# A graph-and-mixture kernel: last scan chunk unpaired, its tail work re-timed, and the spare-tile condition moved ahead of the first mixture

## The chip, the cores and the metric

The kernel runs on one core of one Trainium2 chip. The metric is device time in microseconds (us), the median over timed runs of one launch. A core has five engines, each with a queue of its own that it works through in order: TensorE (PE, matmuls; PEld is its weight load), VectorE (DVE), ScalarE (ACT), GpSimd (POOL) and SyncE (SP, which here only issues transfers). A wait at the head of a queue holds everything behind it.

## The reference

Two layers on 4096 tokens of width 256. Each has a graph part and a mixture of experts, both added to the input. What matters here, cut down:

```python
def step(hst, inp):                       # the scan over the tokens
    dAt, dBut, Ct = inp
    hst = dAt * hst + dBut                # 512 channels x 16 states
    return (hst, hst @ Ct)
y = (ys + u * D_skip) * silu(z)
# layer 0
h = layernorm(relu(adj @ x_n @ gcn_w + gcn_b))
x = x + mamba(h) @ w_out                  # the scan sits in here
xf = layernorm(x)                         # first mixture: 8 experts, the best 2 of each token
probs = softmax(xf @ gate_w + gate_b)
x = x + sum over the best 2:  probs_e * (gelu(xf @ W1_e + b1_e) @ W2_e + b2_e)
# layer 1
x = x + relu(new_adj @ (tanh(x_n @ W_proj + b) @ W_gcn) + b)
x = x + second mixture                    # 6 experts, the best 2, three layers each
```

The reference computes every expert on every token; the kernel only those that were chosen.

## The kernel before

**Stages.** The scan of layer 0 runs first, to about 1296 us of the span; then routing for the first mixture, the first mixture, the propagation of layer 1, the second mixture and the output.

**The scan.** The tokens are cut into 8 chunks of 512. Each chunk takes 32 steps (n = 0 to 255 over all chunks; c is the chunk and i the step in it); a step treats one block of 128 channels and two of the 16 states. In each step POOL forms `db` (L1058), ScalarE the two decays `da` (`decay`, L1066), VectorE runs the two scans (`scan`, L1073) and multiplies by C into `hc` (`product`, L1083). Then the two states are to be summed up. In a *paired* step (`pair`, L1087) POOL issues a transfer that adds the second half of `hc` onto the first, and PE adds one half into the sum `psy` (`total`, L1100). In an unpaired step there is no transfer and PE adds both halves. When a block's last group is in, VectorE multiplies the sum by the gate `zs` (`gate`, L1109). All steps but the last four (252 to 255) are paired. The loop calls `total` for step n-3 and `gate` for step n-4; what is then left over is done after the loop.

**The work that runs beside the scan.** The order of the instructions on PE, VectorE, ScalarE and POOL inside the scan is written out by hand. `Front` prepares the next chunk. From step i = 8 of chunk 6 on, the tails run (`Tail`): for each chunk and each half of it (two token tiles), three steps: product(0), product(1) (L861 and L865, into `ps_out`, for which there is one buffer), then `put`: ScalarE copies the result to `xr` (L870), SP writes it to `x1d`, and ScalarE forms the mean and the squares (L876, L880, reading `ps_out`). `Norm` turns the result into normalised tokens and gate logits, one chunk after the other: fetch, normal (L913), turn (L924, L932) and logits (L936, L940); a piece goes to the steps in `NPIECES` of chunk 7, at `7 + 3 * c + d`. The roots and shifts of the deviations (L893, L902) stand in `NORMS`, at steps 1, 2, 18 and 19. `Last` does the same for chunk 7: `first` at steps 29 and 30, then `add` (L983) and `norm` after the loop (L997 to L1030), where the last logits are copied by L1028 and the residual rows by L1030.

**Routing.** `Dispatch` handles the choice. `choose` (with `router`, L98 to L126) takes the two best experts of each token tile, `place` (L209 to L244) gives every chosen row its place in its expert's list and ends with one-hot rows (L249, eight tiles' worth of columns each). There are two batches of token tiles: the first 28, then the last 4. `tables` (L262 to L348) then makes the number of tiles `d_tiles` (L270), the expert of each tile `d_exps` (L313), the bias of each tile (`d_b`, L332 and L336), the source rows `d_src` (L326) and the destination rows `d_dst` (L348). The second mixture uses the same class with eight batches of 4 tiles.

**The mixtures.** `expert_tiles` runs tiles of 256 rows that belong to one expert. For the first mixture up to 39 tiles can be needed (4096 x 2 rows and 8 experts). Per tile: POOL fetches the rows (`fetch`, L354), SP loads the weights and bias (L452, L455), PE transposes (L459), VectorE copies (`xkT`, L463), PE multiplies (L438), ScalarE applies the function (`hk`, L442), PE multiplies again (L423), VectorE adds the bias (L428) and POOL scatters the rows (`put`, L362). The first 36 tiles always run; the last three stand in a condition behind them:

```python
most = 2 * N // TR + dp.E // 2
tiles = nc.values_load(dp.tiles[0:1, 0:1], min_val=1, max_val=dp.K)   # L480
run(0, most)
with tc.If(tiles > most):                                              # L482
    run(most, dp.K)
```

`combine` (L490, L496) then gathers the two results of each token and adds them with their weights. The second mixture runs 37 tiles and has no condition.

Of the kernel before, what the change touches and what calls it, by code (L numbers as in the profile page):

```python
# [10 lines left out]
BF16 = mybir.dt.bfloat16  # L11
# [7 lines left out]
P = 128  # L19
CW = 512  # L20
TPC = CW // P
# [6 lines left out]
def kernel(ctx: ExitStack, tc: tile.TileContext, out: bass.AP, **a):  # L28
# [115 lines left out]
    def after(later, earlier):  # L144
        tc.add_manual_dep(
            later.ins, earlier.ins.name,
            mybir.DependencyInfo(mybir.DependencyClass.Sync, mybir.DependencyReason.DATA),
            reason="rows written by several transfers",
        )

    class Dispatch:
# [4 lines left out]
        def __init__(self, pool, E, name, batches):  # L156
# [6 lines left out]
            self.hi = pool.tile([P, 2 * NT], F32, name=f"{name}_hi")  # L163
            self.lo = None
            self.src = pool.tile([P, self.C], I32, name=f"{name}_src")
            self.dst = pool.tile([P, self.C], I32, name=f"{name}_dst")
# [33 lines left out]

        def place(self, b, psum, tag, pool, lo_pool):

# [41 lines left out]
            nc.vector.tensor_copy(self.hi[:, g0:g0 + G], rowi)  # L244
            if self.lo is None:
                self.lo = lo_pool.tile([P, 2 * NT, P], BF16, name=f"{self.name}_lo", bufs=1)
            S = 2 * TPC
            for g in range(0, G, S):
# [5 lines left out]
        def tables(self, psum, tp, biases):  # L254
# [70 lines left out]
            nc.vector.tensor_scalar(tok, tok, -1.0, 0.0, ALU.add, ALU.max)  # L325
            nc.vector.tensor_copy(self.src, tok)  # L326

            out = []
            for n, b in enumerate(biases):
                bk = self.pool.tile([P, b.shape[2], K], F32, name=f"{name}_b{n}")  # L330
                for m in range(b.shape[2]):
                    nc.vector.tensor_tensor(  # L332
                        tmp, ge[:, :, :E],
                        b[:, :, m].unsqueeze(1).to_broadcast([P, K, E]), ALU.mult,
                    )
                    nc.vector.tensor_reduce(bk[:, m, :], tmp, AX.X, ALU.add)  # L336
                out.append(bk)
# [44 lines left out]
    class Route:  # L382

        def __init__(self, dp, psum, tags, pool, lo_pool, fm, source, hidden, w, bias_b):
            self.dp, self.psum, self.tags, self.pool, self.lo_pool = dp, psum, tags, pool, lo_pool
            self.source, self.hidden, self.w, self.bias_b = source, hidden, w, bias_b
            self.ps = {}
            self.fm = fm  # L390
# [18 lines left out]
        def choose(self, b):  # L409
            dp, E = self.dp, self.dp.E  # L410
            logits = self.ps.pop(b)[:, :TPC * E].rearrange("p (t e) -> p t e", e=E)
            dp.choose(b, logits, self.bias_b, True, small)
            dp.place(b, self.psum, self.tags[2], small, self.lo_pool)

    def expert_tiles(dp, psum, pool, weights, bias_out, layers, kb_out, spare):
# [62 lines left out]

        most = 2 * N // TR + dp.E // 2
        tiles = nc.values_load(dp.tiles[0:1, 0:1], min_val=1, max_val=dp.K)  # L480
        run(0, most)
        with tc.If(tiles > most):  # L482
            run(most, dp.K)

    def combine(dp, pool, c, src, dst):
# [25 lines left out]
    with ExitStack() as s1:  # L511
# [43 lines left out]
        gate_b = load_bcast(const, a["L0_ffn_gate_b"], "gate_b")  # L555
        dp = Dispatch(r0, E0, "d0", [NT - TPC, TPC])

# [269 lines left out]
        class Tail:  # L827
# [3 lines left out]
            def __init__(self, c, hh, kept=None):  # L831
                self.c, self.hh, self.kept = c, hh, kept
                self.xr = None
                self.todo = [lambda: self.product(0), lambda: self.product(1), self.put]

            @staticmethod
            def step(tails):
                if tails:
                    tails[0].todo.pop(0)()
                    if len(tails) > 1 and tails[1].xr is None:  # L840
                        tails[1].fetch()
                    if not tails[0].todo:
                        tails.pop(0)
# [23 lines left out]
            def put(self):  # L867
                s0 = self.c * TPC + 2 * self.hh
                for j in range(2):
                    nc.scalar.activation(  # L870
                        self.xr[:, j, :], self.ps[:, j, :], AF.Identity,
                        accum_out=sums[:, s0 + j:s0 + j + 1],
                    )
                rows = tokens(x1d[self.c], 0)[:, 2 * self.hh:2 * self.hh + 2, :]
                nc.sync.dma_start(rows, self.xr)
                nc.scalar.activation(  # L876
                    nmean[:, s0:s0 + 2], sums[:, s0:s0 + 2], AF.Identity, scale=-1.0 / D
                )
                for j in range(2):
                    nc.scalar.activation(  # L880
                        self.ps[:, j, :], self.ps[:, j, :], AF.Square,
                        bias=nmean[:, s0 + j:s0 + j + 1], accum_out=ssq[:, s0 + j:s0 + j + 1],
                    )
# [60 lines left out]
        B0 = NT // 2  # L944
        NORMS[18] = lambda: Norm.root(B0, NT - TPC - B0)
        NORMS[19] = lambda: Norm.shift(B0, NT - TPC - B0)
        NPIECES = {}
        for c in range(NC - 1):
            nm = Norm(c)
            for d, piece in ((-2, nm.fetch), (0, nm.normal), (1, nm.turn), (2, nm.logits)):  # L950
                NPIECES.setdefault(7 + 3 * c + d, []).append(piece)

        class Last:
# [34 lines left out]
            def norm(self):  # L988
# [5 lines left out]
                for hh in range(2):  # L994
# [27 lines left out]
                    for j in range(2):  # L1022
                        for k in range(DB):
# [3 lines left out]
                            )  # L1027
                    nc.scalar.copy(lgs[:, s0:s0 + 2, :], ps_l[:, t0:t0 + 2, :])  # L1028
                for hh in range(2):
                    nc.scalar.copy(self.xr[hh], self.ps[hh])  # L1030
                    rows = tokens(x1d[c], 0)[:, 2 * hh:2 * hh + 2, :]
                    nc.sync.dma_start(rows, self.xr[hh])

        class Step:
# [3 lines left out]
            def __init__(self, c, i):  # L1038
# [6 lines left out]

                self.paired = c * STEPS + i < NC * STEPS - 4

# [63 lines left out]
        with tc.manual_schedule(engines={  # L1111
# [34 lines left out]
            advance(left)  # L1146
            steps, tails, kept = [], [], {}
            for n in range(NC * STEPS):
# [32 lines left out]
                cur.product()  # L1181
                if n > 3:
                    steps[n - 4].gate()
                if n > 2:
                    steps[n - 3].total()
                if i < 8:
# [13 lines left out]
            n = NC * STEPS  # L1200
            for k in range(n - 3, n):
                steps[k].total()
            for k in range(n - 4, n):
                steps[k].gate()
# [3 lines left out]
        dp.lo = onehots  # L1208
        dp.choose(0, lgs[:, :NT - TPC, :], gate_b, False, ra)
        dp.place(0, ps_y, "psy", ra, None)  # L1210
        last.norm()
# [5 lines left out]
    with ExitStack() as s2:  # L1217
        with ExitStack() as st:
            tp = st.enter_context(tc.tile_pool(name="tiles0", bufs=2, reuse_waits="tile"))
            with ExitStack() as sr:  # L1220
                rp = sr.enter_context(tc.tile_pool(name="routing0", bufs=2, reuse_waits="tile"))
                ps_r = sr.enter_context(tc.tile_pool(name="ps_r0", bufs=2, space=PSUM, reuse_waits="tile"))
                dp.choose(1, lgs[:, NT - TPC:, :], gate_b, False, ra)
                dp.place(1, ps_r, "pl", ra, None)
                b1 = load(wp, a["L0_ffn_b1"], "b1")
# [31 lines left out]
        eb2 = load(keep1, a["L1_ffn_expert_b2"], "eb2")  # L1257
        dp1 = Dispatch(keep1, E1, "d1", [TPC] * NC)

        def route1(pool, psum, tags, fm):  # L1260
# [4 lines left out]

            return Route(dp1, psum, tags, pool, keep1, fm, x3, hidden, rw2, rb2)

# [254 lines left out]
```

## Time and profile before

| | us |
|---|---|
| median of 3 runs | 2531.24 (2530.56 to 2532.2) |
| the profiled run | 2528.41 |
| its span | 2526.6 |
| PE busy | 2253.9 (89%) |
| VectorE busy | 1652.0 (65%) |
| ScalarE busy | 1196.9 (47%) |
| POOL busy | 1158.9 (46%) |
| accumulating transfers L1087 | x252, 870 ns of POOL each |
| row fetches L354 / scatters L362 | x146 / x146 (two for each tile, both mixtures) |
| granted clock of PE, mean | 0.941 |

The span is the time from the first to the last instruction that the profile shows; the run is 1.8 us longer. A page of the profile gives for each group its line, engine, operation, tiles (out<-in) and shape, then how often it ran, its busy time, the mean of one and the engine's idle time before it with what ended it. A row of the timeline begins with the start and the duration; in brackets at its end stand the idle time of the engine before it and what released it. Where one row stands for several instructions (x2), the duration is that of all of them.

### The profile page before, as it was taken

What the parts mean: (1) busy time and instruction counts of PE and PEld (TensorE: products, weight loads), DVE (VectorE), ACT (ScalarE), POOL (GpSimd) and SP (SyncE); (2) the same over time, 40 slices, a digit from 0 to 9 for tenths busy, and PEclk for the clock granted to TensorE, in tenths of its full rate; (3) what the DMA queues carried; (4) which work ended last, traced back from release to release, by engine and by line L of the source; (5) the groups of instructions that cost most, each with busy time, mean ns of one, the idle gap of its engine ahead of it and who ended that gap; (6) DMA issues with size and microseconds to landing.
All of it is one profiled execution on the core that took longest, in us unless ns stands there. A gap on an engine that the chain in (4) does not pass through costs nothing. (4 is left out here: it accounts for less than half of the span.)

```text
span 2526.6 us, 25781 instructions
## 1 busy us (share of the span) xinstructions
PE 2253.9 (89%) x7976; PEld 1453.3 (58%) x7976; DVE 1652.0 (65%) x2322; ACT 1196.9 (47%) x2029; POOL 1158.9 (46%) x861
## 2 busy tenths in 40 slices
PE   5989999999999999897876999789999999859991
PEld 4765655656465656554545888645444444448881
DVE  4049999999999999978994111292666666552224
ACT  1146656574656566675632222154666665423330
POOL 1037776777777777756733555310000000026650
PEclk9999999999999999998877999899999999969996
DMA  6369999999899999988955777561444444238776
GB/s 201 92 185 234 242 265 234 264 231 271 221 270 230 259 247 238 270 242 224 283 156 183 235 228 233 168 211 50 142 142 142 142 148 147 98 113 246 245 241 212
DMA packets 307185, 516.91 MB, mean 205 GB/s; under 512 B 25808, under 2 KB 174928, under 8 KB 306144
## 3 DMA queue, kind: packets, MB, share of 16 engines
q1 hardware_dynamic: 256736, 410.81, 51.3%
q0 software_dynamic: 50304, 104.37, 19.8%
q8 instruction: 67, 1.10, 0.2%
q14 instruction: 78, 0.64, 0.1%
HBM read 406.29 MB, written 42.73 MB: 178 GB/s over the span
## 5 line engine op out<-in xcount | busy, mean ns | idle before, releaser
L1058 POOL TENSOR_TENSOR db<-du,bb 128x1024 f32<-128x1024 f32 x256 | 606.7, 2370 | 345.5 <-ACT state L1079 125.7
L1073 DVE TENSOR_TENSOR_SCAN db<-da,state,db 128x512 f32<-128x512 f32 x512 | 627.4, 1266 | 55.6 <-ACT da L1066 53.2
L613 PE MATMUL pt<-at,gn 128*128 128x256 f32 x2048 | 492.7, 393 | 33.2 <-DVE gn L80 26.2
L1066 ACT ACTIVATE da<-dt,negA 128x512 f32<-128x512 f32 x512 | 347.6, 691 | 360.2 <-DVE db L1073 358.1
L613 PEld LDWEIGHTS pt<-at,gn 128*128 128x128 f32 x2048 | 401.4, 197 | 164.4 <-issue 73.3
L1316 PE MATMUL pf<-f,gn 128*128 128x512 f32 x1024 | 449.4, 594 | 0.0
L1083 DVE TENSOR_TENSOR hc<-db,cb 128x1024 f32<-128x1024 f32 x256 | 331.6, 1295 | 18.4 <-PE psy L1100 0.4
L1316 PEld LDWEIGHTS pf<-f,gn 128*128 128x128 f32 x1024 | 191.8, 190 | 227.3 <-issue 226.4
L1100 PE MATMUL psy<-hc,ident 128*128 128x512 f32 x520 | 279.7, 624 | 41.7 <-DMA hc<-hc 40.9
L442 ACT ACTIVATE hk<-ps_h,d_b 128x256 f32<-128x256 f32 x292 | 138.4, 474 | 370.2 <-PE ps_h L438 352.7
L78 POOL TENSOR_TENSOR ln_rs<-ln_rs,mhalf 128x4 f32<-128x4 f32 x24 | 34.5, 1436 | 573.5 <-DVE ln_rs L77 573.5
L428 DVE TENSOR_TENSOR yk<-ps_y,bk 128x512 f32<-128x512 f32 x73 | 50.5, 692 | 376.1 <-PE ps_y L423 327.0
L1306 ACT ACTIVATE f<-f 128x1024 f32<-128x1024 f32 x128 | 135.4, 1058 | 200.2 <-DVE f L1305 177.4
L354 POOL DMA_INDIRECT xk<-d_xd,d_src x146 | 141.8, 971 | 190.7 <-PE ps_xt L459 82.3
L1087 POOL DMA_DIRECT2D hc<-hc x252 | 219.3, 870 | 0.2
L438 PE MATMUL ps_h<-xkT,wk 128*128 128x256 f32 x872 | 212.5, 387 | 0.0
L423 PE MATMUL ps_y<-wk,hk 128*128 128x256 f32 x872 | 210.4, 379 | 0.1
L1305 DVE TENSOR_SCALAR f<-at 128x1024 f32<-128x1024 f32 x128 | 88.1, 689 | 170.1 <-PE pf L1316 163.2
L362 POOL DMA_INDIRECT d_ys<-yk,d_dst x146 | 144.0, 987 | 109.6 <-DVE yk L428 75.8
L438 PEld LDWEIGHTS ps_h<-xkT,wk 128*128 128x128 f32 x872 | 161.3, 192 | 32.4 <-ACT hk L442 11.2
L423 PEld LDWEIGHTS ps_y<-wk,hk 128*128 128x128 f32 x872 | 162.9, 190 | 21.2 <-ACT hk L442 0.5
L1100 PEld LDWEIGHTS psy<-hc,ident 128*128 128x128 f32 x520 | 99.5, 198 | 105.4 <-DVE db L1073 38.1
(236 smaller groups left out, 2503.7 us busy)
## 6 DMA issues: line engine op xcount, KB each, us to landing
at<-in_adjT_dram SPq DMA_DIRECT2D x256, 512.0 KB, 4.1
bb<-bcd SPq DMA_DIRECT2D x128, 512.0 KB, 5.3
cb<-bcd SPq DMA_DIRECT2D x128, 512.0 KB, 5.0
hc<-hc POOLq DMA_DIRECT2D x252, 256.0 KB, 6.4
wk<-in_L_ffn_W_dram SPq DMA_DIRECT2D x72, 512.0 KB, 4.9
wk<-in_L_ffn_expert_w_dram SPq DMA_DIRECT2D x111, 256.0 KB, 4.1
yg<-d_ys SPq DMA_DIRECT2D x32, 512.0 KB, 5.1
yd<-us SPq DMA_DIRECT2D x6, 1024.0 KB, 8.1
```

The costliest lines, as they stand in the source:

```text
L354: nc.gpsimd.indirect_dma_start(out=xk[:, j, :], out_offset=None, in_=self.xd[:, :], in_offset=bass.IndirectOffsetOnAxis(ap=self.src[:, c:c ...
L362: s_ = nc.gpsimd.indirect_dma_start(out=self.ys[:, :], out_offset=bass.IndirectOffsetOnAxis(ap=self.dst[:, c:c + 1], axis=0), in_=yk[:, j, ...
L423: nc.tensor.matmul(ps[:, j, :], hT[:, m, j * P:(j + 1) * P], w[:, m, :], start=(m == 0), stop=(m == kb_out - 1),)
L438: nc.tensor.matmul(ps[:, j, :], w[:, d, m * P:(m + 1) * P], xT[:, d, :], start=(d == 0), stop=(d == DB - 1),)
L613: nc.tensor.matmul(pt[:, k, :], xl[:, j, k * P:(k + 1) * P], at[:, jj, :], start=(j == 0 and k == 0), stop=(j == NT - 1 and k == DB - 1),)
L1058: nc.gpsimd.tensor_tensor(self.db, self.f.du[self.half][:, self.mi:self.mi + 1, :].to_broadcast([P, 2, CW]), self.bb, ALU.mult,)
L1066: nc.scalar.activation(da, self.f.dt[self.half][:, self.mi, :], AF.Exp, scale=negA[:, self.m, n:n + 1])
L1073: nc.vector.tensor_tensor_scan(self.db[:, j, :], da, self.db[:, j, :], state[:, self.m, n:n + 1], ALU.mult, ALU.add,)
L1083: nc.vector.tensor_tensor(self.hc, self.db, self.cb, ALU.mult)
L1087: nc.gpsimd.dma_start(self.hc[:, 0, :], self.hc[:, 1, :], accum_op=ALU.add)
L1100: nc.tensor.matmul(f.psy[m], ident, self.hc[:, j, :], start=False, stop=(self.g == GS - 1 and j == last),)
L1316: nc.tensor.matmul(pf[:, k, :], gn[:, j, k * P:(k + 1) * P], f[:, jj, :], start=(j == 0), stop=(j == NT - 1),)
```

## The change

It has these parts:

1. No step of chunk 7 is paired. The totals of unpaired steps run up to step n-2 instead of n-3, and a gate is called one step after its total.
2. The mean and squares of a tail (`Tail.squares`) run at the start of the next call of `Tail.step`, that is one step later, behind that step's decays.
3. The second root and shift go from steps 18 and 19 to 19 and 20, and the pieces of `Norm` three steps later.
4. The batches of the first mixture are 24 and 8 token tiles instead of 28 and 4. The one-hot rows are a function of their own, called for both batches after the second `place`.
5. In `tables` the bias products are ordered behind `d_src`, in both mixtures.
6. In `Last.norm` the residual copies are ordered behind the copies of the logits.
7. In the first mixture 35 tiles always run, and the condition with the four spare tiles stands ahead of the first of them. The list of scatters that later work is ordered behind starts anew after it.

```diff
-        def place(self, b, psum, tag, pool, lo_pool):
+        def place(self, b, psum, tag, pool):
...
-            if self.lo is None:
-                self.lo = lo_pool.tile([P, 2 * NT, P], BF16, name=f"{self.name}_lo", bufs=1)
-            S = 2 * TPC
+            self.row[b] = row
+
+        def one_hot(self, b):
+            g0, G, S, row = 2 * self.t0[b], 2 * self.T[b], 2 * TPC, self.row.pop(b)
             for g in range(0, G, S):
...
-            nc.vector.tensor_copy(self.src, tok)
+            found = nc.vector.tensor_copy(self.src, tok)
...
-                    nc.vector.tensor_tensor(
+                    mul = nc.vector.tensor_tensor(
...
+                    if n == 0 and m == 0:
+                        after(mul, found)
...
-        most = 2 * N // TR + dp.E // 2
+        most = 2 * N // TR + dp.E // 2 - 1
         tiles = nc.values_load(dp.tiles[0:1, 0:1], min_val=1, max_val=dp.K)
-        run(0, most)
         with tc.If(tiles > most):
             run(most, dp.K)
+        dp.sent = []
+        run(0, most)
...
-        dp = Dispatch(r0, E0, "d0", [NT - TPC, TPC])
+        dp = Dispatch(r0, E0, "d0", [NT - 2 * TPC, 2 * TPC])
...
+            rest = []
             @staticmethod
             def step(tails):
+                while Tail.rest:
+                    Tail.rest.pop()()
...
                 nc.sync.dma_start(rows, self.xr)
+                Tail.rest.append(self.squares)
+
+            def squares(self):
+                s0 = self.c * TPC + 2 * self.hh
                 nc.scalar.activation(
                     nmean[:, s0:s0 + 2], sums[:, s0:s0 + 2], AF.Identity, scale=-1.0 / D
                 )
...
-        NORMS[18] = lambda: Norm.root(B0, NT - TPC - B0)
-        NORMS[19] = lambda: Norm.shift(B0, NT - TPC - B0)
+        NORMS[19] = lambda: Norm.root(B0, NT - TPC - B0)
+        NORMS[20] = lambda: Norm.shift(B0, NT - TPC - B0)
...
-                NPIECES.setdefault(7 + 3 * c + d, []).append(piece)
+                NPIECES.setdefault(10 + 3 * c + d, []).append(piece)
...
-                    nc.scalar.copy(lgs[:, s0:s0 + 2, :], ps_l[:, t0:t0 + 2, :])
+                    done = nc.scalar.copy(lgs[:, s0:s0 + 2, :], ps_l[:, t0:t0 + 2, :])
                 for hh in range(2):
-                    nc.scalar.copy(self.xr[hh], self.ps[hh])
+                    after(nc.scalar.copy(self.xr[hh], self.ps[hh]), done)
...
-                self.paired = c * STEPS + i < NC * STEPS - 4
+                self.paired = c < NC - 1
...
-                if n > 3:
-                    steps[n - 4].gate()
-                if n > 2:
-                    steps[n - 3].total()
+                for k in gated:
+                    steps[k].gate()
+                gated = []
+                while summed < n - 1 and (summed < n - 2 or not steps[summed].paired):
+                    steps[summed].total()
+                    gated.append(summed)
+                    summed += 1
...
-                dp.choose(1, lgs[:, NT - TPC:, :], gate_b, False, ra)
-                dp.place(1, ps_r, "pl", ra, None)
+                dp.choose(1, lgs[:, dp.T[0]:, :], gate_b, False, ra)
+                dp.place(1, ps_r, "pl", ra)
+                for b in range(2):
+                    dp.one_hot(b)
```

`after(later, earlier)` orders one instruction behind another.

## The prediction, made before the changed kernel ran

> **What bounds the kernel now.** The profiled run took 2528.41 us, 1.8 around a span of 2526.6; the median of the three timed runs is 2531.24, 2.8 above it. The sum below is in differences, and I add it to the median. Four stages matter: scan with its last chunk (to 1296.5), routing (to 1347.7, the first fetch), first mixture (to 1634), second mixture (to 2476). I read first the busy time by stretch, for the last two scan chunks and for the middle of the first mixture:
> ```profile
> 1034.65:1156.34 121.69, 104.79 (x315) 61.23 (x313) 104.20 (x95) 81.90 (x181) 78.77 (x49) 0.91 0.89 238
> 1156.34:1296.55 140.21, 115.26 (x404) 76.10 (x405) 125.11 (x110) 86.23 (x212) 102.09 (x62) 0.82 0.89 244
> ...
> 1590.00:1610.00 20.00, 20.00 (x100) 17.36 (x99) 3.87 (x6) 4.49 (x10) 6.02 (x7) 1.00 0.65 209
> ```
> After the stretch and its length come PE, PEld, DVE, ACT and POOL busy, then the granted clock. In the last chunk VectorE leads (125 of 140 us), but PE is close at 115, at a clock of only 0.82. In the mixture PE is busy all the time: only fewer tiles help there.
>
> Next, who waits for whom from 1115 to 1297 (the total, times, the longest):
> ```profile
> ACT lgs L940 <- PE ps_lg L936: 21.0, 7, 4.2
> PEld ps_out L861 <- ACT ps_out L880: 17.6, 6, 5.2
> DVE db L1073 <- ACT da L1066: 17.3, 7, 5.8
> PE psy L1100 <- DMA hc<-hc: 14.7, 10, 4.7
> ...
> PE ps_out L861 <- ACT ps_out L880: 12.5, 5, 4.4
> ```
> VectorE stops for ScalarE's `da`; ScalarE is late because it works, in order, for PE; and PE waits for ScalarE's squares (L880) and for the summed halves. How one such stop comes about, from the timeline:
> ```profile
> 1187.87 0.45 ACT L880 ACTIVATE ps_out<-ps_out,x_mean 128x256 f32<-128x256 f32 x1
> 1188.24 0.19 ACT L880 ACTIVATION_READ_ACCUMULATOR ps_out<-ps_out,x_mean 128x1 f32 x1
> 1188.33 1.29 ACT L1066 ACTIVATE da<-dt,negA 128x512 f32<-128x512 f32 x2
> 1188.54 1.02 PE L1100 MATMUL psy<-hc,ident 128*128 128x512 f32 x2
> 1189.12 2.46 DVE L1073 TENSOR_TENSOR_SCAN db<-da,state,db 128x512 f32<-128x512 f32 x2 [3.24 <-ACT da L1066]
> ```
> The squares stand ahead of the next `da`, and the scan has stood idle 3.24 us.
>
> At the end of routing, the rows on VectorE and the fetch on POOL:
> ```profile
> 1342.37 0.70 DVE L332 TENSOR_TENSOR tb_tmp<-tb_ge,b 128x312 f32<-128x312 f32 x1
> 1343.37 0.32 DVE L320 COPY tb_inv<-ps_inv 128x156 f32<-128x156 f32 x1 [0.30 <-PE ps_inv L297]
> ...
> 1347.24 0.20 DVE L326 CAST d_src<-tb_tok 128x78 int32<-128x78 f32 x1
> ```
> ```profile
> 1347.72 1.09 POOL L354 DMA_INDIRECT xk<-d_xd,d_src  x1 [37.74 <-DVE d_src L326]
> ```
> Last, the first mixture's end:
> ```profile
> 1622.27 0.69 DVE L428 TENSOR_TENSOR yk<-ps_y,bk 128x512 f32<-128x512 f32 x1 [6.09 <-PE ps_y L423]
> ...
> 1625.72 0.69 DVE L428 TENSOR_TENSOR yk<-ps_y,bk 128x512 f32<-128x512 f32 x1 [2.76 <-PE ps_y L423]
> ...
> 1627.97 0.97 POOL L362 DMA_INDIRECT d_ys<-yk,d_dst  x1 [0.31 <-issue]
> ...
> 1634.03 0.93 SPq L490 DMA_DIRECT2D yg<-d_ys  x2
> ...
> 1637.94 2.46 DVE L496 SCALAR_TENSOR_TENSOR x<-yg,d_wv,x 128x256 f32<-128x256 f32 x6 [10.64 <-DMA yg<-d_ys]
> ```
> The last put is issued by 1628.94, but the gather leaves at 1634.03.
>
> **One tile fewer: -7.4.** L428 of earlier tiles starts at 1600.15, 1607.52, 1614.90, 1622.27: 7.37 us a tile, PE full. This holds if the inputs need at most 35 tiles. Worked out from the reference's inputs, the eight experts get 1034, 1175, 881, 1013, 1024, 941, 988 and 1136 tokens, so 5+5+4+4+4+4+4+5 = 35 tiles of 256 rows: just enough, and one more token for the fifth expert would make 36.
>
> **Condition away from the end: -2.2.** At L482 POOL's queue waits for the puts to 1631.6 (4206 ns), then spends 2092 ns on INC_SWDGE_SEM. The first is the landing and stays; the second goes. The gather then leaves at about 1631.8 instead of 1634.03; bounds -2.1 (that row alone) and -2.3.
>
> **The condition at its new place: 0.** Each engine reads the tile count (481 ns on SP, 719 on DVE at L480), branches, and passes its semaphores. Cover: POOL idles 37.74 us before the first fetch, PE 11.59 and ACT 15.24 before their first work; SP has nothing until the experts' numbers (d_exps, 1342.28), which VectorE writes long after the count (1328.01). SP's nine semaphores took 1609.1 to 1612.1, so with the read some 3.6 us, against 14 free (with the x2 loads it also waits for, at least 5). Without cover it would cost 3.6 (SP) to 6.2 (if POOL also had its 2092 ns on this path). The Trainium skill speaks against the move ("Runtime: NRT & Kernel Launch", Instruction fetch mechanics): a taken branch to a page that is not held fetches it by DMA before going on. It gives no price, so by it the sum is worse by an unstated amount wherever there is no cover; the row nearest is DVE's 0.53 us idle after L482.
>
> **Accumulating halves dropped in the last chunk: +1.2.** 28 of 252 L1087 go from POOL (0.87 us each, off the path), and with them most of PE's 14.7 us on hc<-hc. PE gets 28 more L1100 passes at 0.86 us a pass at full speed: 28 x 0.86 = 24 us. It had 115 busy of 140 at clock 0.82; VectorE needs at least 32 x (2.45 + 1.23) = 117.8, and with gates, norms and roots some 126. So PE still fits, but it is late at the chunk's first gates, where L725 stands behind L1095 and now two more pairs of L1100. The stop of 3.24 at 1189.12 grows by at most the 1.72 of one pair. Bounds: -3.0 (the three last stops, 0.93, 0.94 and 1.17, at 1259.78, 1272.22, 1283.58, come with a slow PE and vanish) and +1.7; I take +1.2, as the first stop is certain and L725 hides part of the pair. The skill says PE's clock falls after idle windows of about 3.4 us ("TensorE: Matmul & The Clock Gate", What's actually happening); by that rule more matmuls keep it fast, and the sum is -10.6 instead of -6.4. The 0.82 agrees, but which gaps close no row shows.
>
> **Squares a step later: +1.4.** From step 200 on there are 14 halves of tail (7 chunks, two each), three steps a half. Each time L876 and L880 (1.3 us, 1187.03 to 1188.33) leave the way of a `da`: gain at most 14 x 1.3 = 18.2. But the one buffer of ps_out comes free after two `da` (2 x 0.69 = 1.4) instead of before: the next L861 waits longer, and behind it on PE, in order, stand L1100 and L725, for which ScalarE and then VectorE wait: loss at most 14 x 1.4 = 19.6. Both are the same queue seen from its two ends; I take the difference, +1.4, and keep -18.2 and +19.6 as far bounds. Half of these is likely enough to count.
>
> **Norms over later steps: 0.** Root and shift move by one step, the pieces by three, in the same number. Last.first still runs at 29 and 30. Bounds: -1.7 and +1.2, the neighbouring stops (1.74 at 1209.26; 1.2 on lgs).
>
> **Routing: +2.0.** The instruction order puts both last gates (L1109, 0.68 each) behind the first choice instead of into it; the norm of the last tiles, and the last logits, come some 1.6 later: 1318.2 instead of 1316.67. Before, seven one-hots (8.03 us, from 1311.86) covered that wait and L98 came at 1319.80: -1.6. But four of the one-hots now stand between L98 and L109, inside the second choice's dependent chain: 4 x 1.15 - 0.3 (the wait on L107 they fill) = +4.3. One more stands behind the second place: +1.15. The second batch is twice as wide, 64 columns for 32: about +0.6. Then L326 is no longer behind four bias pairs: from L320 (1343.37) seven short rows of some 0.22 give d_src at 1344.9 instead of 1347.44: -2.5. Sum -1.6+4.3+1.15+0.6-2.5 = +2.0; bounds 0.4 (logits not late) and 4.5 (src gains nothing). Last.norm's copies behind the logits delay x1d's write and the x2 loads behind it on SP by about 5.5 us; they land some 10 us ahead of the first weights' issue.
>
> **Second mixture: -1.4.** There, too, three bias pairs (about 0.6 each with what is between) stand ahead of d_src. Its fetch starts 2.06 after d_src, which the profile puts down to a landing of bk; the fetch reads nothing of bk, but bounds are 0 and -1.4. I take the gain.
>
> Sum: -7.4-2.2+0+1.2+1.4+0+2.0-1.4 = -6.4. Forecast 2531.24-6.4 = **2524.8**.
>
> **Rivals.** (1) *The scan's stops vanish.* For: the squares stand right ahead of `da` in the rows shown; 17.3 us of stops. Against: their waits begin on PE. With two thirds of them gone, -11.5 replaces +2.6: 2510.7. (2) *The late buffer wins.* PE, with 24 us more work, waits at each L861 and carries it to L725 and `da`. For: 30.1 us of PE and PEld waits on L880 already. Against: before, a half takes three steps and more of 4 us, and the loop of squares, products, copies and `da` about 12 us. Each half that pays costs 1.4: without the term +1.4 the sum is -7.8, so from 10 of 14 on (+14, sum +6) the kernel is slower by more than 5.1. With 12: 2531.24-7.8+16.8 = 2540.2. (3) *36 tiles.* If rounding moves one token to the fifth expert, all four spare tiles run: 39 instead of 36, 4 x 7.37 = 29.5 more than in the forecast, plus draining and refilling PE (4.2 us landing, and 11.0 from a fetch at 1347.72 to L438 at 1358.72): 2524.8+29.5+15.2 = 2569.5. Against: the smallest gap of logits that would do it is about 5e-5 at a spread of 0.33.
>
> **How the numbers follow.** A measurement of this kernel tells about 0.2% (5.1 us) from no change: below 2526.2 is faster, above 2536.3 slower. Forecast 0.55, its own range 2518 to 2531 (routing and first bounds), of which 0.32 faster and 0.23 no change; rival 1: 0.19, faster; rival 2: 0.18, of which 0.14 slower and 0.04 no change; rival 3: 0.08, slower. So faster 0.51, the same 0.27, slower 0.22. The range, 2509 to 2540, leaves out rival 3 and the ends of 1 and 2.
>
> **What would show it.** Right: 35 L428 in the first mixture, one cadence less; a gather some 3 us after the last put's issue; d_src next to L320; one-hots between L98 and L109. Wrong: steps 200 to 242 longer than 203 us with PE waiting for L880 (rival 2), no stops on `da` (rival 1), x152 in the indirect fetches where 35 tiles give x144 (rival 3).

## The result: no change, and the profile after

The changed kernel took 2530.07 us in the median of 12 runs (2526.24 to 2534.76), the kernel before 2530.22 in 12 (2522.06 to 2534.7). The ratio is 1.0006, with a 95% interval of 0.9992 to 1.002: no change that can be measured. The forecast was 2524.8, 0.25% faster. The range, 2509 to 2540, held the time; the case that was called the likeliest, a faster kernel, did not come.

Runs of one and the same program lie up to 12.6 us apart here (the kernel before), so a stage says more than a total. Both kernels were profiled twice (the second time as the experiments before_again and changed_again), and this is where the time lies. The table goes by milestones of the traces; apart from product 255, which is taken at its end, each is the start of an instruction:

| stretch, us | before | before, again | after | after, again | mean difference |
|---|---|---|---|---|---|
| start of product 224 to end of product 255 | 137.66 | 137.12 | 136.96 | 137.57 | -0.1 |
| end of product 255 to the first row fetch | 51.17 | 51.22 | 55.97 | 55.48 | +4.5 |
| first row fetch to the last bias addition (L428, now L434), first mixture | 278.00 | 276.19 | 274.26 | 274.66 | -2.6 |
| last bias addition to the first gather | 8.31 | 8.34 | 5.59 | 5.62 | -2.7 |
| first gather to d_exps of the second mixture | 607.34 | 609.14 | 608.57 | 608.90 | +0.5 |
| d_exps to the last bias addition, second mixture | 234.69 | 235.01 | 233.50 | 234.57 | -0.8 |

So the change did what it says in the mixture: one tile less, and a gather that leaves earlier behind the last scatter. But routing took 4.5 back, the mixture lost about half of the saved tile again at its start (from the first fetch to the first bias addition 27.7 and 28.1 us, where it was 23.9 and 22.1), and the last chunk of the scan, in which most was moved, came out even. The stages add up to -1.2 us; the medians differ by -0.15, which the spread of the runs allows.

The busy time by stretch in the kernel after, the second row being the last chunk:

```profile
1034.95:1156.65 121.70, 98.30 (x311) 58.91 (x309) 105.99 (x96) 81.50 (x181) 78.78 (x49) 0.92 0.91 237
1156.65:1296.14 139.49, 122.79 (x446) 75.77 (x446) 124.51 (x110) 85.90 (x210) 80.79 (x34) 0.91 0.61 192
```
PE has 122.8 us of work instead of 115.3, at a clock of 0.91 instead of 0.82; POOL lost the accumulating transfers (102.1 to 80.8). VectorE's work is the same, and the chunk is as long as before.

Who waits for whom from 1115 to 1297, after:

```profile
PEld ps_out L873 <- ACT ps_out L896: 22.0, 7, 6.0
ACT lgs L956 <- PE ps_lg L952: 18.1, 7, 3.2
PE ps_out L873 <- ACT ps_out L896: 15.5, 7, 4.4
DVE db L1089 <- ACT da L1082: 13.8, 10, 3.9
...
ACT zs L746 <- PE ps_xz L733: 7.6, 4, 3.7
```
Before, the same stretch had 17.3 us of VectorE's stops for `da`, 17.6 and 12.5 of the weight load's and PE's waits for the squares (L880, now L896) and one wait of ScalarE for L725 (now L733), 2.3 us. So VectorE's stops fell to 13.8, the waits for the squares rose to 22.0 and 15.5 (the two rows are largely the same stops, seen on the weight load and on the multiplication), and ScalarE now waits four times for L733, the products of the last chunk's own gate `zs`.

The end of routing after, on VectorE:

```profile
1302.34 0.69 DVE L1125 TENSOR_TENSOR us<-psy,zs 128x512 f32<-128x512 f32 x1 [1.28 <-PE psy L1116]
1304.05 0.69 DVE L1125 TENSOR_TENSOR us<-psy,zs 128x512 f32<-128x512 f32 x1 [1.03 <-PE psy L1116]
...
1319.89 0.23 DVE L98 TENSOR_TENSOR rt_lg<-lgs,gate_b 128x64 f32<-128x64 f32 x1 [2.67 <-ACT lgs L1044]
1320.03 1.22 DVE L252 TENSOR_TENSOR gn<-iota,pl_row 128x1024 bf16<-128x1024 f32 x1
...
1334.29 0.13 DVE L273 CAST d_tiles<-tb_ct 1x1 int32<-1x1 f32 x1
...
1349.45 0.32 DVE L323 COPY tb_inv<-ps_inv 128x156 f32<-128x156 f32 x1 [0.72 <-PE ps_inv L300]
...
1351.03 0.20 DVE L329 CAST d_src<-tb_tok 128x78 int32<-128x78 f32 x1
```
The last gates (L1125, formerly L1109) wait for PE and start 6.2 and 5.7 us after the last product in the two profiles, where they started 2.7 after it; VectorE stops 2.67 us for the last logits and then does four one-hots (L252) inside the chain behind them. `d_src` follows L323 by 1.6 us, where it was 3.9.

The end of the first mixture after:

```profile
1626.37 0.69 DVE L434 TENSOR_TENSOR yk<-ps_y,bk 128x512 f32<-128x512 f32 x1 [2.76 <-PE ps_y L429]
...
1628.62 0.97 POOL L367 DMA_INDIRECT d_ys<-yk,d_dst  x1 [0.30 <-issue]
...
1631.96 0.93 SPq L498 DMA_DIRECT2D yg<-d_ys  x2
```
2.4 us from the last issue to the gather, where there were 5.1.

The start of the first mixture after: SP's queue, then PE's first work, then the branch on SP and on VectorE (counts, then the durations in ns and the first and last start).

```profile
1349.89 1.06 SPq L458 DMA_DIRECT2D wk<-in_L_ffn_W_dram  x2
1356.77 0.35 SPq L461 DMA_DIRECT2D bk<-in_L_ffn_b_dram  x1
1358.07 0.97 SPq L458 DMA_DIRECT2D wk<-in_L_ffn_W_dram  x2
```
```profile
1356.84 1.34 PE L465 MATMUL ps_xt<-ident,xk 128*128 128x128 f32 x5 [7.43 <-DVEq L488]
```
```profile
L488 SPq COMPARE_BRANCH  x1: 50/50/50, 1335.3 to 1335.3; - x1
...
L488 DVEq COMPARE_BRANCH  x1: 72/72/72, 1356.5 to 1356.5; - x1
```
SP passed the branch from 1335.3 to 1337.6, in idle time, as the prediction had it. VectorE, with all the tables ahead of it in its queue, reached it only at 1356.5. Right after that, and not before, SP issued the first tile's bias and PE began. The bias is the one that costs, as the first experiment shows.

### The profile page after: what moved, and what is told of

Read it like the earlier page. It is cut to its first block, busy times and chain, and to the rows that moved or that the text cites. A ratio compares the mean times of both kernels' runs of the same rounds, so it can differ in the third digit from the quotient of the medians.

```text
span 2524.9 us, 25719 instructions
## 1 busy us (share of the span) xinstructions
PE 2254.3 (89%) x7996; PEld 1446.3 (57%) x7996; DVE 1652.4 (65%) x2320; ACT 1194.0 (47%) x2025; POOL 1133.7 (45%) x829
## 5 line engine op out<-in xcount | busy, mean ns | idle before, releaser
L1116 PE MATMUL psy<-hc,ident 128*128 128x512 f32 x576 | 301.6, 619 | 33.2 <-DMA hc<-hc 33.1
L434 DVE TENSOR_TENSOR yk<-ps_y,bk 128x512 f32<-128x512 f32 x72 | 49.8, 692 | 364.8 <-PE ps_y L429 317.7
L367 POOL DMA_INDIRECT d_ys<-yk,d_dst x144 | 142.1, 987 | 121.7 <-DVE yk L434 87.7
L1103 POOL DMA_DIRECT2D hc<-hc x224 | 195.1, 871 | 0.2
L1116 PEld LDWEIGHTS psy<-hc,ident 128*128 128x128 f32 x576 | 110.7, 197 | 110.3 <-issue 60.2
```

The source lines that it names most:

```text
L367: s_ = nc.gpsimd.indirect_dma_start(out=self.ys[:, :], out_offset=bass.IndirectOffsetOnAxis(ap=self.dst[:, c:c + 1], axis=0), in_=yk[:, j, ...
L1103: nc.gpsimd.dma_start(self.hc[:, 0, :], self.hc[:, 1, :], accum_op=ALU.add)
L1116: nc.tensor.matmul(f.psy[m], ident, self.hc[:, j, :], start=False, stop=(self.g == GS - 1 and j == last),)
```

## The experiments

Each experiment is the changed kernel with the edit shown; the edits are cut to the lines that matter. Durations are from the profile of each run, and "steps 224 to 255" and the other stretches are those of the table above; the tile count is d_tiles (L273), counted from the end of product 255. Runs without an interval were timed once.

### Bias buffers of their own for the spare tiles

```diff
-            bk = pool.tile([P, D], F32, name="bk", bufs=3)
+            bk = pool.tile([P, D], F32, name=f"bk{own}", bufs=2 if own else 3)
...
-            run(most, dp.K)
+            run(most, dp.K, "_own")
```

> The changed kernel with one edit: the four spare tiles load their bias into buffers of their own. Theory (the first tile outside the condition reuses a bias buffer of a spare tile, so SP's bias load waits until VectorE has passed the branch, and the next tiles' weights stand behind it on SP): the first bias load is issued within 1.5 us of the first weights instead of 6.9 behind them; the stretch from the first row fetch to the last L434-type bias addition falls from 274.3 us to about 270.7 (before: 278.0 with 36 tiles, less 7.37). Rival (PE starts slowly because the rows land late): that stretch stays within 0.7 us of 274.3. Time of a run: 3.5 us less under the theory, the same under the rival.

SP's queue at the start of the mixture:

```profile
1351.65 1.06 SPq L458 DMA_DIRECT2D wk<-in_L_ffn_W_dram  x2
1352.95 0.92 SPq L461 DMA_DIRECT2D bk<-in_L_ffn_b_dram  x1
1354.83 0.97 SPq L458 DMA_DIRECT2D wk<-in_L_ffn_W_dram  x2
```
The bias goes out 1.3 us behind the first weights (6.9 in the changed kernel), and the stretch from fetch to last bias addition took 270.2 us instead of 274.3. One run took 2524.48. VectorE reached the branch no sooner (1358.2) and PE began no sooner (1359.92, behind the rows' landing), so PE's late beginning was not what cost. The theory holds: a spare tile's bias addition on VectorE releases the buffer that the first tile outside the condition loads into. When the condition isn't taken, VectorE still has to pass the branch before that buffer counts as free, and SP, in order, holds the following weights behind the bias: the third tile's weights went out 8.9 us after the first fetch in the changed kernel (1360.98) and 3.0 after it here (1356.85).

### The condition back behind the tiles

```diff
+        run(0, most)
         with tc.If(tiles > most):
             run(most, dp.K)
-        dp.sent = []
-        run(0, most)
```

> The changed kernel with the condition put back behind the 35 tiles. Theory: the start of the mixture is as in the kernel before (fetch to last bias addition 270.7 us instead of 274.3), and the end costs what it did: from the end of the last scatter's issue to the first gather's issue 5.1 us instead of 2.4. Net 1 us less than the changed kernel. Rival (the move was free at the start): 274.3 stays and the end is 2.7 longer, net 2.7 more.

The stretch was 270.9 us, and from the last bias addition to the gather it took 7.25 instead of 5.59 (8.3 in the kernel before): 3.3 gained, 1.7 lost, where 2.7 lost was expected. 2527.74 in one run. So the move as made cost more at the start than it gave at the end, and the first experiment shows that the cost isn't the condition itself but the bias buffers that it shares with the tiles outside.

### The first batch's one-hots right after its place

```diff
         dp.place(0, ps_y, "psy", ra)
+        dp.one_hot(0)
...
-                for b in range(2):
-                    dp.one_hot(b)
+                dp.one_hot(1)
```

> The changed kernel with the six one-hots of the first batch called right after its place, as before, and two behind the second place. Theory (VectorE's stop of 2.67 us ahead of L98 is left open because four of the one-hots went behind it): the stop goes to 0 and the tile count is ready 35.8 us after the last product of the scan instead of 38.2; first fetch 2.4 earlier. Rival (the logits bound the chain, and one-hots between its links are free): the second batch's chain starts 1.8 later and the tile count comes within 0.6 us of 38.2.

VectorE there:

```profile
1315.74 6.89 DVE L252 TENSOR_TENSOR gn<-iota,pl_row 128x1024 bf16<-128x1024 f32 x6
1322.56 0.22 DVE L98 TENSOR_TENSOR rt_lg<-lgs,gate_b 128x64 f32<-128x64 f32 x1
1323.61 0.22 DVE L108 TENSOR_REDUCE rt_red<-rt_lg 128x8 f32<-128x64 f32 x1 [0.32 <-ACT rt_lg L107]
```
The stop ahead of L98 is gone, and the tile count came 36.3 us after the last product instead of 38.2: 1.8 of the 2.4 expected. Some of the rest went into small waits inside the chain (0.32 here on L107) that the one-hots had filled. 2525.95 in one run.

### The scan's three parts, one by one

Five runs put parts 1, 2 and 3 back in different combinations, with all else as changed; the second profiles of both kernels fill two corners, though the kernel before also differs in the routing. Where part 1 is undone, the last four steps, unpaired in every kernel, keep the new order of the totals. The edits:

```diff
-                self.paired = c < NC - 1
+                self.paired = c * STEPS + i < NC * STEPS - 4
```
```diff
-                Tail.rest.append(self.squares)
+                self.squares()
```
```diff
-        NORMS[19] = lambda: Norm.root(B0, NT - TPC - B0)
-        NORMS[20] = lambda: Norm.shift(B0, NT - TPC - B0)
+        NORMS[18] = lambda: Norm.root(B0, NT - TPC - B0)
+        NORMS[19] = lambda: Norm.shift(B0, NT - TPC - B0)
...
-                NPIECES.setdefault(10 + 3 * c + d, []).append(piece)
+                NPIECES.setdefault(7 + 3 * c + d, []).append(piece)
```

The second edit alone:

> The changed kernel with mean and squares back inside the same step's put. My step for them was a net of two ends, +1.4: then steps 200 to 255 take 1.4 less than the 257.4 us of the changed kernel. Rival 1 of the prediction (the squares' delay of the decays is what costs): 5 us or more longer. Rival 2 (the late buffer costs): 5 us or more shorter.

All three:

> The changed kernel with parts 1, 2 and 3 undone (steps paired up to 251, squares in put, norms at their old steps); routing and mixtures as changed. Control: steps 224 to 255 take the 137.7 us of the kernel before within 0.7. If the lateness of the last logits comes from part 3 or 1, the last gates run as before, and the tile count is ready about 35.5 us after the last product instead of 38.2; if it comes from the split of the batches alone, 38.2 stays.

The second and third:

> The changed kernel with parts 2 and 3 undone, part 1 (last chunk unpaired) kept. With squares_back (134.2 us for steps 224 to 255, norms late) this tells part 1 from part 3. If dropping the halves is what gains: 134.2 within 0.7. If the later norms gain: 137.7. My step for part 1 said +1.2, that is 138.9. For the end: if the norms' three steps make the last gates late, the first last gate starts 2.7 us after the last product starts to end as before, instead of 6.2, and the tile count is ready at 35.5 instead of 38.2; if unpairing does, 38.2 stays.

The first alone:

> The changed kernel with part 1 alone undone (paired up to 251, squares late, norms late). If part 1 gains 3.5 by itself, steps 224 to 255 take 140.5 us instead of 137.0; if part 1 is neutral, 137.0 within 0.7; by my step for part 1 (+1.2) 135.8.

The first and second:

> The changed kernel with parts 1 and 2 undone, part 3 (norms later) kept. Fourth corner: paired with late squares took 133.0 us for steps 224 to 255, unpaired with squares in put 134.2, unpaired with late squares 137.0. If PE's lateness is what each of the two edits costs, and either alone is absorbed, this one takes 132 to 134; if the edits are independent (each +3 to +4), 130.3. If the later norms gain only together with one of them, 137.7 as before.

None of them, on both kernels:

> The kernel before, profiled a second time, to see how far stages of the same program differ: steps 200 to 224 and 224 to 255 within 1 us of 121.7 and 137.7, first fetch to last bias addition 278.0, first gather of the first mixture to the second mixture's expert numbers within 2 us of 607.3 (the changed kernels show 608.6 to 610.8). If steps 200 to 224 differ by 3 us as two of the other kernels did (118.5), differences of that size in that stretch say nothing of an edit.

> The changed kernel, profiled a second time: 121.7 and 137.0 for the two stretches of the scan within 1 us, tile count 38.2 us after the last product, first fetch to last bias addition 274.3.

Steps 224 to 255, in us:

| norms | squares | paired up to 251 | last chunk unpaired |
|---|---|---|---|
| early (before) | in put (before) | 137.7, 137.1 (before, twice), 139.4 (scan_before) | 137.7 (unpaired_only), 136.9 (combined) |
| late (changed) | in put (before) | 128.3 (paired_sq_back) | 134.2 (squares_back) |
| late (changed) | a step later (changed) | 133.0 (paired_again), 132.9 (combined_paired) | 137.0, 137.6 (after, twice), 137.5, 136.7, 136.8 (first three experiments) |

Late norms with the squares a step later is the change's own row; early norms with late squares isn't valid, as the roots would read squares that aren't there yet. The later norms gain 9 us in the chunk by themselves against the kernel before and 11 against scan_before, which has the changed routing too (3 where the chunk is unpaired). Late squares cost 4.7 with paired steps and 2.8 with unpaired ones; with late norms, dropping the pairs costs 5.9 with the squares in put and 4.0 with late ones. With early norms it costs nothing that shows (137.7 and 136.9 beside 137.1 to 139.4). Together the two eat the whole gain. paired_sq_back, squares_back and unpaired_only were profiled once each, and the three profiles at the upper left, with one and the same scan, lie 2.3 apart: the 2.8 and the 3 are near what one profile can tell, the larger figures are well above it.

For the chunk most expectations missed: squares_back lay between mine and rival 2, paired_again outside all three, and paired_sq_back 2.0 below its lowest; unpaired_only's 137.7 is the one that was given for the later norms as what gains. Of the second profiles, changed_again came as expected; before_again had 118.6 for steps 200 to 224 instead of 121.7 and 276.2 for the mixture instead of 278.0. The control, scan_before, missed too: 139.4 where 137.7 within 0.7 was expected. Its rows show why. With the first batch of 24 tiles and early norms the first choice (L98) starts 25.3 us ahead of the end of product 255, where it started 13.0 ahead before, and VectorE waits there for the logits 4.1 us instead of 1.2.

VectorE's stops in scan_before, at steps 233, 235 and 238 and at the first choice:

```profile
1203.34 2.46 DVE L1089 TENSOR_TENSOR_SCAN db<-da,state,db 128x512 f32<-128x512 f32 x2 [2.77 <-ACT da L1082]
1212.84 2.46 DVE L1089 TENSOR_TENSOR_SCAN db<-da,state,db 128x512 f32<-128x512 f32 x2 [1.68 <-ACT da L1082]
1226.41 2.46 DVE L1089 TENSOR_TENSOR_SCAN db<-da,state,db 128x512 f32<-128x512 f32 x2 [2.06 <-ACT da L1082]
...
1276.71 0.36 DVE L98 TENSOR_TENSOR rt_lg<-lgs,gate_b 128x192 f32<-128x192 f32 x1 [4.07 <-ACT lgs L956]
```
In paired_sq_back, with the norms late and all else the same, step 233 has 0.80, steps 235 and 238 have no stop, and L98 waits 0.16:

```profile
1196.67 2.46 DVE L1089 TENSOR_TENSOR_SCAN db<-da,state,db 128x512 f32<-128x512 f32 x2 [0.80 <-ACT da L1082]
...
1273.40 0.36 DVE L98 TENSOR_TENSOR rt_lg<-lgs,gate_b 128x192 f32<-128x192 f32 x1 [0.16 <-ACT lgs L956]
```
These four stops make up 9.6 of the 11.0 us. Up to step 241 the tails run, and with early norms the pieces of the first three chunks stand at steps 231 to 239, among them. That this overlap is what makes the stops fits the rows but was not tried by itself; nor were the roots (one step) and the pieces (three) moved apart.

The cost of the late squares shows in the waits: in the last chunk PE waits for L896 14.0 us in paired_again and 4.5 in paired_sq_back, and VectorE for `da` 9.9 and 3.9. It also shows ahead of the chunk. Steps 200 to 224, where the tails run and no other part of the scan's change acts, took 118.5 to 118.9 us in four profiles and 121.7 to 122.0 in three with the squares in put, but 121.7 to 122.1 in six and 125.5 in one with late ones. On average that is 2.4 more. The two values with squares in put differ by a single stop of VectorE for `da`, at step 219, of 2.69 or 5.83 us in one and the same program; what decides between them was not found.

The last chunk of paired_sq_back, busy time and then the waits of its stretch from 1155.38 to 1286.23:

```profile
1155.38:1286.23 130.85, 109.61 (x387) 69.84 (x387) 124.25 (x110) 85.85 (x210) 102.62 (x62) 0.81 0.94 261
```
```profile
PE psy L1116 <- DMA hc<-hc: 7.9, 8, 1.8
...
PE ps_out L873 <- ACT ps_out L896: 4.5, 2, 2.9
...
DVE db L1089 <- ACT da L1082: 3.9, 2, 3.1
```
One row of paired_again (1157.38 to 1292.95), and one of the changed kernel (1156.64 to 1296.14):

```profile
PE ps_out L873 <- ACT ps_out L896: 14.0, 5, 4.3
```
```profile
DVE db L1089 <- ACT da L1082: 11.6, 7, 3.9
```
VectorE, with 124 us of work, needs 131 for it. PE has the slower clock (0.81) and still waits for the halves, and the chunk is the shortest all the same: VectorE stops for `da` only twice, 3.9 us. In the same stretch of the changed kernel it stops seven times, 11.6 us.

The stretch behind the scan gives part of this back. With early norms the tile count came 35.2 us (scan_before) and 35.4 (unpaired_only) after the last product, with late ones 37.7 to 38.5 in all runs that keep the changed routing. The first last gate starts 3.2 and 3.7 after the last product with early norms, 5.7 to 6.5 with late ones. By the order of the program the last piece of logits then sits at step 30, and PE does it, and `Last`'s products, ahead of the last sums.

### Two versions

combined: bias buffers, squares in put, norms early, first one-hots early, unpaired.

> The changed kernel with what the first four runs favour: spare tiles' bias in own buffers, squares back in put, norms at their old steps (valid only with the squares back), the first batch's one-hots right after its place. Terms against the changed kernel: -3.8 (fetch to last bias addition), -2.8 (steps 224 to 255), -1.8 (one-hots) and 0 to -2.7 (last logits, if the norms made them late). Sum -8.4 to -11.1, so 2519 to 2522 where the changed kernel has 2530. If the parts of the scan don't add (norms at the old steps take the gain back), 2525.

2519.64 us (6 runs), ratio 0.9957 to the kernel before (0.994 to 0.9974). The sum came as expected, but not by its terms: the chunk stayed at 136.9, as the early norms took the gain back, the tile count was ready 33.0 after the last product, 5 earlier than in the changed kernel, and steps 200 to 224 took 118.9, some 3 less.

combined_paired: bias buffers, first one-hots early, paired; squares and norms late.

> The changed kernel with part 1 undone, the spare tiles' bias in own buffers and the first batch's one-hots right after its place (squares and norms late as changed). Against combined (2519.6): chunk 133.0 instead of 136.9 (-3.9), tile count 36.3 instead of 33.0 after the last product (+3.3, late last gates): 2519 within 2. If the last gates are no later because PE is ahead, 2516.

2524.67 us (12 runs), ratio 0.9974 (0.9963 to 0.9985), outside the expected 2519 within 2. The chunk had its 132.9, but the tile count came at 37.6 instead of 36.3 (the first last gate only 7.6 after the last product), and steps 200 to 224 took 125.5 where other runs have 118.5 to 122.1. Why they did was not found.

Both are faster than the kernel before, timed beside them, by less than half a percent; the changed kernel was not timed beside them. The fastest single run of all is paired_sq_back with 2516.91, which has neither the bias buffers nor the early one-hots. Whether these three together are better still was not tried.

## Why the prediction was partly right

The time lay within the range, but that says little of the working: the range is 31 us wide, and of the forecast's gain of 6.4 us the stages show 1.2. The mixture gave 4.3 less than forecast, routing cost 2.5 more, the second mixture and the stretch before it 1.1 more, and the scan 2.7 less, by luck, as its terms show.

**One tile fewer, -7.4: right**, and so was the count of 35 tiles (144 row fetches instead of 146, both mixtures together). With the start put right it shows: 278.0 and 276.2 before, 270.2 in own_bk and 270.9 in cond_last.

**Condition away from the end, -2.2: right**, -2.7 by the stage and -1.7 by cond_last.

**The condition at its new place, 0: wrong, and the step that cost the forecast most.** The prediction weighed the branch on POOL, PE, ScalarE and SP against each engine's own idle time, and for SP, among the first to pass, the cover was there. What it missed is that an engine that passes late holds the others: bias buffers used in the condition become free for SP only when VectorE has gone by, and VectorE, for which no cover was worked out, has none, because it comes to the branch with all the tables behind it, at 1356.5. Price: 4.1 us by own_bk (274.3 to 270.2), 3.3 by cond_last.

**Accumulating halves dropped, +1.2: too small, and right in sign only with late norms.** It costs 4.0 to 5.9 there and nothing that shows with early ones. The prediction weighed PE's 24 us against its free time and let the first stop grow by at most 1.72 us. That place was right: with unpaired steps ScalarE waits 6.7 to 7.6 us for L733, with paired ones 0.5 to 2.3, and the longest stop of VectorE for `da` grew from 3.1 (paired_sq_back) to 5.3 us (squares_back), 2.2; with the smaller stops, they came to 8.6 us instead of 3.9. Of the three late stops that were to vanish with a slow PE, the one at 1283.58 is no stop for `da` but L98's wait for logits. The Trainium skill ("TensorE: Matmul & The Clock Gate", What's actually happening) states that idle windows throttle the clock and activity releases it. The trace agrees, in that the clock rose from 0.82 to 0.91 with the further sums, but the gain drawn from it did not come: the shortest chunk ran at 0.81.

**Squares a step later, +1.4: right in sign, too small**, 2.8 to 4.7 in the chunk and, as an average over runs that differ, some 2.4 ahead of it. Of the two ends of the queue the late buffer is the heavier: PE's waits on L896 rose, and VectorE's stops for `da` rose with them instead of falling.

**Norms later, 0: wrong**, -9 to -11 in the chunk and about +2.8 behind it. The bounds were -1.7 and +1.2, taken from neighbouring stops. The pieces were seen as the same work three steps on; that the steps of the tails then hold fewer of them, and that the first choice then starts later, was not worked out. So the scan's sum, +2.6, was near the measured -0.1 by compensation, not by its terms.

**Routing, +2.0: mis-sized**, +4.5. The one-hots behind L98 and the wider batch came as worked out (L98 to d_tiles 14.4 us instead of 8.2, +6.2 where +6.05 was said), and so did d_src, 2.3 us closer to L323 where 2.5 was said. The last logits were 3.1 to 3.6 us later after the last product instead of 1.6; with early norms they were 0.6 to 0.8 later, so most of it is the norms' doing. And the fetch follows `d_src` by 0.88 instead of 0.28 in every changed kernel; no run settles the latter.

**Second mixture, -1.4: not shown**, -0.8 on average, but the changed kernels' profiles have 233.5 to 235.3 us for this stretch and the kernel before 234.7 and 235.0. The fetch came 2.5 to 3.1 earlier behind d_exps, but the tiles after it took 2 longer: the first products start 14.8 us after d_exps, where it was 14.9 and 15.6, so the rows' fetch alone does not set the start.

The rivals: of the stops of rival 1 (-11.5) about half went where part 3 stood alone (8.7 us were left of 17.3), but through the norms and not, as the rival had it, through the squares. Rival 2, the late buffer and the busier PE, is what parts 1 and 2 did. Its 30.1 us of waits counted the same stops twice, on PE and on its weight load. The sign set for it came: from product 200 to product 242 it took 205.7 and 206.1 us, with longer waits for the squares; the mark of 203 was what the kernel before itself took (203.2, and 200.4 the second time). Each rival was given as an alternative; a part of each was at work at once.

## What to carry to other kernels

A branch that was not taken still ordered engines here: a buffer used inside became free outside only when the engine that would have read it had passed, so look for the engine that comes latest, not for the one whose own queue is idle, and give the branch buffers of its own. When a change has several parts in one tightly coupled loop, an even sum says nothing of its terms: put each part back by itself before keeping any. And ahead of a change that makes an engine busier or a buffer free later, ask what stands behind it in that engine's order; here 28 more sums on PE, 24 us by the prediction's price, fitted easily and still cost 4 to 6 us where the norms were late.

## What the runs showed of the hardware

Profiles of the same program differ by stretch. Up to step 200 all kernels here have the same order of work, and product 200 started between 1035.9 and 1044.1 us of the span in the fourteen profiles. Steps 200 to 224 took 118.6 and 121.7 in the two of the kernel before, by one stop of VectorE, while the last chunk of the changed scan repeated within 0.9 in five profiles and the path from last product to tile count within 0.8 in four. In the two pairs of profiles of one kernel, 4.3 of 5.3 us and 5.7 of 6.5 us of the difference in span lie ahead of product 224. So a difference of 3 us in the last chunk or in routing can mostly be read from one profile; in steps 200 to 224, or in the total, it can't.

A higher granted clock of PE did not go with a shorter chunk: 0.81 at 128.3 us (paired_sq_back), 0.91 at 137.0 (after).
